# A block-matching convolution kernel: residual addition behind side work, 5x5 convolution in 64x64 tiles, another order of the first image's prologue

## The chip, the cores and the metric

The kernel runs on one core of a Trainium2 chip, as one launch. A core has a matrix engine (TensorE, PE in the profile, with its weight loads as PEld), a vector engine (VectorE, DVE), a scalar engine (ScalarE, ACT), a general engine (GpSimd, POOL) and a queue engine (SyncE, SP). DMAs are issued from POOL, SP or ACT. The engines run their own instruction streams in order and wait for each other through semaphores. The metric is the device time of one execution in microseconds. Before the change it is 6942.3 us, the median of three runs (6939.84 to 6943.18).

## The reference

Eight images of 32 channels and 128x128 pixels, all in f32. Two layers, each of them with a group normalisation ahead and a residual addition behind:

```python
# layer 0
x = x + L0(_gn(x), ...)
# layer 1
x = x + L1(_gn(x), kernel5x5)

def L0(x):
    xb = _patch_match_stack(x)          # for each pixel the 8 best of 25 offsets
                                        # (3x3 patch distance), 8 shifted copies: 256 channels
    dct = _conv(xb, dct_w, groups=C)
    h = relu(_conv(_conv(xb, w1), w2, groups=CK, pad=1))   # 1x1 256->256, depthwise 3x3
    h = relu(_conv(_conv(h, w3), w4, groups=CK, pad=1))
    wiener = sigmoid(_conv(_conv(h, w5), w6, groups=CK, pad=1))
    filt = _conv(wiener * dct, inv_dct_w, groups=C)
    return _conv(filt, agg_w)

def L1(x):                              # one 5x5 kernel for every channel
    return conv(x.reshape(B * C, 1, H, W), kernel, padding=2).reshape(x.shape)
```

`_gn` has 16 groups of two channels: it subtracts the mean of a group and divides by its standard deviation, which is known only when all pixels of the group are there.

## The kernel before

The work is a list of `steps`, (b, n) for image b = 0 to 7 and row group n = 0 to 16. A step s runs, in this order, i = 3, 2, 1, 0: the third 1x1-and-depthwise pair of an older step, the second of the step before, the first of the current step, and the end of the oldest one. For i of 1 to 3, `pointwise_v` makes the half of the 1x1 convolution whose depthwise part is done on DVE (`depthwise_v`: 8 taps of scalar_tensor_tensor on 128x1024, L695, behind a first tap by ACT, L692), and `pointwise_t` makes the half whose depthwise part is done on PE (`depthwise_t`, L718), with DMAs `t<-t` between them. For i = 0, `final_dct` multiplies by the dct of the gathered patches (64x64 matmuls into the two tiles `pc`, L777, then DVE at L785), and `final_add` multiplies by the merged inverse dct and aggregation (`pa`, L798), adds the residual on DVE (L805), takes the statistics of the result (L806) and writes it to `x1d` in DRAM (L810).

Beside these, a step gathers the patches of coming steps in four units. A unit is `gather_load` (DMAs of indices `ib` and of pixels `xt`, issued by POOL), `gather_select` (two ACT operations for each of a number of pairs, L588 and L589) and `gather_pixels` (88 small matmuls `pg`, L603). A unit needs the indices of its quarter of the rows: `ready` holds (b, quarter).

PE, DVE and ACT have a hand-written order: what the Python code emits first runs first. DMAs of POOL and SP are placed by a scheduler. Side work is written as generators, which yield a queue's letter, a cost and, in some places, a number of ticks to wait: "D" work is done by `tick`, four times a step, as far as a credit goes (`total`, spread over the steps of an image); "P", "Q" and "A" are drained at fixed places of the loop; `until` drains all of them until a condition holds. The side work of an image is:

- `prep(b)`: load image b (`load_image`), normalise it (`xn`), form squared differences for the offsets (`df`, L414 and L422, cost `PAIR`), sum over channels (`pd`, L429), sum over patches (`dsum`), take the top 8 (`mx`, `idx`, L506 and L507), turn them to gather indices (`o`, `pi`, `li`, L529 to L540; DRAM tile `idxd`), quarter by quarter.
- `mixes()` and `bands()`, once: matrices made from the small weights (`dq`, `iv`, `ag`, `ldct`, `ib`, `lagg`) and from the 5x5 kernel (`band`, five 128x128 band matrices, one for each dx).
- `layer1(b)`: statistics (L818), then for each of eight chunks of four channels a load `xy` from `x1d` (L837), the normalisation into `xm` (L842, four tensor_scalar), five matmuls `p5` with `band` (L861; an f32 matmul is two instructions), the addition (L872) and the write-out (L873). Two `xy` buffers take turns.

Before the first step, seven gather units are loaded, four of them completed, and a unit of index 3 or less belongs to quarter 0, one of 4 to 7 to quarter 1. Image 0's loads are issued by ACT; SP loads the constants `cst` and all weights. The transposes of w1, w3 and w5 for the 1x1 convolutions are made in a set-up block, in their own PSUM tiles. After it, PSUM has the pools `ps_x` (five banks, tag "x", for pv, p, pg, pc, pa and p5 among others), `ps_dw` and `ps_d`.

In the loop, the `pa` matmuls and the residual addition stand together, after `pointwise_v` of i = 3 in the step that follows:

```python
later()                        # end(): final_add, at the last step of an image push(layer1(b))
later = lambda: None
...
run("Q")
if s < len(steps):
    unit(gather_select, u + 1, (0,))
    unit(gather_load, u + 3)
    tick(b, i)
next(new_v, None)              # taps of depthwise_v on DVE
```

Of the kernel before, what the change touches and what calls it, by code (L numbers as in the profile page):

```python
# [9 lines left out]
F32 = mybir.dt.float32  # L10
# [3 lines left out]
ALU = mybir.AluOpType  # L14
ORDERED = {mybir.EngineType.PE, mybir.EngineType.DVE, mybir.EngineType.Activation}

P = 128
C, K, H, W = 32, 8, 128, 128
# [25 lines left out]
def bm3d_conv_preact(  # L44
# [32 lines left out]

    def load_image(b, engine):

        xn = xnp.tile([P, HR, HX], F32, name=f"xn_{b}", tag="xn")  # L80
        for rg in range(4):
            s = slice(C * rg, C * (rg + 1))
            lo = 32 * rg - 3
            a, z = max(lo, 0), min(lo + HR, H)
            engine.dma_start(xn[s, a - lo : z - lo, 2 : 2 + W], x[b, :, a:z, :])
            for r in range(HR):
                y = lo + r
                if y < 0 or y >= H:
                    y = min(max(y, 0), H - 1)
                    engine.dma_start(  # L90
                        xn[s, r : r + 1, 2 : 2 + W], x[b, :, y : y + 1, :]
                    )
        return xn

    first = load_image(0, nc.scalar)
    cst = const.tile([P, C_N], F32, name="cst")
# [50 lines left out]

    with tc.tile_pool(name="setup", bufs=1) as sp, tc.tile_pool(
        name="setup_ps", bufs=2, space=bass.MemoryType.PSUM
    ) as spp:  # L150
        dwt = sp.tile([P, 3, 4, 9], F32, name="dwt")
        for n, w in enumerate((w2, w4, w6)):
            for g in range(4):
                nc.sync.dma_start(
                    dwt[C * g : C * (g + 1), n],
                    w[:P].rearrange("(q c) o a b -> c q (o a b)", c=C),
                )
            nc.gpsimd.memset(dwd[0:C, n, 1], 0.0)
            for u in range(2):
                for dy in range(3):  # L160
                    s = slice(C * (u + dy), C * (u + dy + 1))
                    nc.gpsimd.tensor_tensor(
                        dwd[s, n, u],
                        cst[s, C_M32 : C_M32 + C]
                        .unsqueeze(1)
                        .unsqueeze(1)
                        .to_broadcast([C, 4, 3, C]),
                        dwt[s, n, :, 3 * dy : 3 * dy + 3].unsqueeze(3).to_broadcast([C, 4, 3, C]),
                        ALU.mult,
                    )  # L170
        wide = {}
        for name, w in (("w1", w1), ("w3", w3), ("w5", w5)):
            t = sp.tile([P, 2, CK], F32, name=f"nat_{name}", tag=f"nat_{name}")
            nc.sync.dma_start(t, w.rearrange("(m p) i a b -> p m (i a b)", p=P))
            if name == "w1":

                nat, t = t, sp.tile([P, 2, CK], F32, name="w1_kc")
                for m in range(2):
                    nc.vector.tensor_copy(
                        t[:, m].rearrange("p (k c) -> p k c", c=C),  # L180
                        nat[:, m].rearrange("p (c k) -> p k c", k=K),
                    )
            wide[name] = t
        for name, dst in (("w1", lw1), ("w3", lw3), ("w5", lw5)):
            for g in range(2):
                ps = spp.tile([P, CK], F32, name=f"ps_{name}_{g}", tag="ps")
                for m in range(2):
                    src = wide[name][:, m, g * P : (g + 1) * P]
                    nc.tensor.transpose(ps[:, m * P : (m + 1) * P], src, ident)
                nc.scalar.copy(dst[:, g], ps)  # L190

# [31 lines left out]
    def run(which, credit=1e9):  # L223

        q, took = queues[which], 0.0
        for _ in range(len(q) if which != "D" else 1000):
# [7 lines left out]
                None,  # L234
            )
            if i is None or took >= credit:
                break
# [16 lines left out]
    def group_stats(mv, name):  # L254
# [19 lines left out]
        return mr  # L274

    def mixes():

# [7 lines left out]
        m8 = work.tile([P, 8], F32, name="m8", tag="m16", bufs=1)  # L285
        yield "D", 1.0
        nc.vector.tensor_reduce(
# [224 lines left out]
    def places(b, idx, i):  # L512
# [4 lines left out]
        yield "D", 2.6  # L517
        o = work.tile([P, 256], F32, name=f"o_{b}_{i}", tag="lin_o", bufs=1)
        ct = work.tile([P, 256], F32, name=f"cn_{b}_{i}", tag="lin_c", bufs=1)
        nc.vector.tensor_copy(  # L520
# [266 lines left out]
    def final_add(b, n, acc, xr, j0, j1):  # L787
# [6 lines left out]
        for m in range(2):  # L794
            for j in range(4):
# [7 lines left out]
                    stop=m == 1,  # L803
                )
        nc.vector.tensor_add(xr, xr, pa)  # L805
        nc.vector.bn_stats(stats[b][:, n], xr)  # L806
# [7 lines left out]
    def layer1(b):  # L814
# [15 lines left out]
        bc = work.tile([P, 2, C], F32, name=f"bc_{b}", tag="bc")  # L830
        nc.scalar.copy(bc.rearrange("p a b -> p (a b)"), pb[:, : 2 * C])
        xys = {}

        def load(c):
            if c < C:
                xys[c] = work.tile([P, 4, W], F32, name=f"xy_{b}_{c}", tag="xy")
                nc.gpsimd.dma_start(xys[c], x1d[b][c : c + 4].rearrange("c y x -> y c x"))  # L837

        def normalise(c):
            xm = work.tile([P, 4, W], F32, name=f"xm_{b}_{c}", tag="xm")  # L840
            for i in range(4):
                nc.vector.tensor_scalar(  # L842
                    xm[:, i],
                    xys[c][:, i],
                    bc[:, 0, c + i : c + i + 1],
                    bc[:, 1, c + i : c + i + 1],
                    op0=ALU.subtract,
                    op1=ALU.mult,
                )
            return xm  # L850

        load(0)
        load(4)
        yield "D", 1.4
        xm = normalise(0)
        for c in range(0, C, 4):
            yield "P", 0
            ps = ps_x.tile([P, 4, W], F32, name=f"p5_{b}_{c}", tag="x")
            for n, dx in enumerate((0, -2, -1, 1, 2)):
                xa, xz = max(0, -dx), min(W, W - dx)  # L860
                nc.tensor.matmul(  # L861
                    ps[:, :, xa:xz],
                    band[:, dx + 2],
                    xm[:, :, xa + dx : xz + dx],
                    start=n == 0,
                    stop=n == 4,
                )
            yield "D", 2.1
            if c + 4 < C:
                xm = normalise(c + 4)  # L870
            xy = xys.pop(c)
            nc.vector.tensor_add(xy, xy, ps)  # L872
            nc.gpsimd.dma_start(out[b, c : c + 4].rearrange("c y x -> y c x"), xy)  # L873
            load(c + 8)

        done.add(b)

# [25 lines left out]
    def end(b, n, xr, j0, j1):  # L903
        final_add(b, n, accs.pop((3, b, n)), xr, j0, j1)
        if n == NS:
            push(layer1(b))

    total = 5.5 + 3.3 + 36 * 1.95 + 4 * 4.6 + 32 * 1.85 + 4 * 2.6 + 8 * 2.1
    owed = [0.0]
# [16 lines left out]
    with tc.manual_schedule(engines=ORDERED):  # L926
        push(prep(0))
        push(mixes())
        xbd[0] = dram.tile([P, 2, H, W], F32, name="xbd_0", tag="xbd")
        for i in range(3):  # L930
            nc.gpsimd.memset(tb[i][0:64, :, 0], 0.0)
        for u in range(7):
            unit(gather_load, u)
            unit(gather_select, u - 2)
            unit(gather_pixels, u - 3)
        u = 4

        dt = dv = kept = iter(())

        later = lambda: None  # L940

        for s in range(len(steps) + 2):
            if s < len(steps):
# [6 lines left out]
                if n == NS - 1 and b + 1 < NB:  # L950
                    until(lambda: b + 1 in ready, 4.0)
                    xbd[b + 1] = dram.tile([P, 2, H, W], F32, name=f"xbd_{b+1}", tag="xbd")
            for i in (3, 2, 1, 0):
                si = s - (i - 1 if i else 2)
# [5 lines left out]
                if live and i:  # L960
# [3 lines left out]
                    accs[i, bi, ni] = [None, next(new_v)]  # L964
                later()
                later = lambda: None
                if live and not i:
# [7 lines left out]

                run("Q")
                if s < len(steps):
                    unit(gather_select, u + 1, (0,))
                    unit(gather_load, u + 3)
                    tick(b, i)  # L980
                next(new_v, None)
                if live and i:
                    pointwise_t(i, bi, ni, lws[i - 1], src)
                next(kept, None)
                if s < len(steps):
                    unit(gather_pixels, u)
                next(dt, None)
                run("A")
                next(dv, None)
                if s < len(steps):  # L990
                    unit(gather_select, u + 1, (1,))
                    u += 1
                next(dt, None)
                kept, dv, dt = dv, new_v, new_t
                if live and not i:
                    later = partial(end, bi, ni, xr, j0, j1)
                if not i and 0 <= s - 1 < len(steps):
                    fins[s - 1] = final_load(*steps[s - 1])
        next(kept, None)
        later()  # L1000
        until(lambda: NB - 1 in done, 4.0)

# [61 lines left out]
```

## Time and profile before

| | us |
|---|---|
| median of three runs | 6942.3 |
| profiled execution | 6939.75 |
| its span, first to last instruction | 6938.0 |
| PE busy | 6488.0 (94%) |
| DVE busy | 5777.4 (83%) |
| ACT busy | 5067.6 (73%) |
| POOL busy | 3018.7 (44%) |
| DVE at L805 waiting for `pa` | 581.2 in 109 waits |
| L861, 640 instructions of the 5x5, busy | 327.6 |
| layer-1 statistics L818, first and last | 1132.8 and 6858.8 |
| first `xbd` write (a step's gathered patches) | 206.8 |

Times in the profile count from the start of the span. A busy share is an average over the span; the row of tenths by slices shows where an engine is full. A wait is listed with the instruction that waited, the one that released it, the total in us, the number of waits and the longest. The granted TensorE clock averages 0.976 over the span.

### The profile page before, as it was taken

How to read it: one execution, taken by the hardware profiler on the slowest of the kernel's cores; microseconds unless marked ns; L12 is line 12 of the kernel's file. 1: busy time of each engine (PE TensorE's matmuls, PEld its weight loads, DVE VectorE, ACT ScalarE, POOL GpSimd, SP SyncE). 2: the span in 40 equal slices, each digit the busy share in tenths (PEclk: the TensorE clock that was granted, in tenths of full speed). 3: DMA queues.
4: the chain of work that ended last, by engine and by line, in shares of the span. 5: the costliest groups of instructions: out<-in, count | busy, mean ns of one | idle time of the engine just before them, and what ended most of it. 6: DMA issues, size and time to landing. Idle time of an engine off the chain costs nothing.

```text
span 6938.0 us, 230820 instructions
## 1 busy us (share of the span) xinstructions
PE 6488.0 (94%) x100450; PEld 3042.2 (44%) x100450; DVE 5777.4 (83%) x8606; ACT 5067.6 (73%) x6698; POOL 3018.7 (44%) x5143
## 2 busy tenths in 40 slices
PE   4699999999999999999999999999999999999997
PEld 1344444444444444444444444444444444444443
DVE  6689988889888898888988898888988889877775
ACT  4687778777687777877777776877768777776772
POOL 6345436334463344534445334553435433333332
PEclk9799999999999999999999999999999999999998
DMA  3566656557565575656756567565666666556652
GB/s 79 132 149 148 156 141 160 147 147 161 144 154 148 137 166 133 162 144 142 162 134 164 142 144 163 142 161 137 152 149 147 165 142 143 143 151 154 156 143 66
DMA packets 774196, 1007.83 MB, mean 145 GB/s; under 512 B 223712, under 2 KB 587168, under 8 KB 773184
## 3 DMA queue, kind: packets, MB, share of 16 engines
q0 software_dynamic: 387104, 733.70, 42.1%
q1 hardware_dynamic: 381056, 256.86, 17.2%
q8 instruction: 791, 12.96, 0.8%
q10 hardware_dynamic: 5024, 2.49, 0.2%
q14 instruction: 221, 1.81, 0.1%
HBM read 542.24 MB, written 217.01 MB: 109 GB/s over the span
## 4 chain that ended last, share of the span: by engine, by line
PE 48%; DVE 23%; issue 8%; DMA 8%; ACT 7%; POOL 5%; SPq 0%; POOLq 0%; DVEq 0%; ACTq 0%
PE pw L718 17%; DVE acc L695 16%; PE pv L641 12%; PE p L665 9%; PE pg L603 3%; PE p L861 3%; DMA t<-t 2%; DVE df L414 2%; PE pc L777 2%; DMA xf<-xbd 2%; DVE idx L507 2%; ACT ib L588 1%; PE pa L798 1%; ACT df L422 1%; DMA dsum<-sq 1%
## 5 line engine op out<-in xcount | busy, mean ns | idle before, releaser
L695 DVE SCALAR_TENSOR_TENSOR acc<-tv,dwv,acc 128x1024 f32<-128x1024 f32 (+3 forms) x3264 | 4031.9, 1237 | 242.1 <-ACT acc L692 126.5
L718 PE MATMUL pw<-t,dwd 96*32 96x508 f32 (+6 forms) x19392 | 2162.2, 592 | 84.7 <-DMA t<-t 58.5
L574 POOL DMA_DIRECT2D ib<-idxd x1024 | 566.7, 554 | 2185.9 <-ACT sel L589 2050.3
L718 PEld LDWEIGHTS pw<-t,dwd 96*32 96x32 f32 (+1 forms) x19392 | 712.3, 112 | 1216.7 <-issue 1135.5
L588 ACT ACTIVATE ib<-ib,nplace 128x1024 bf16<-128x1024 bf16 x1024 | 1170.6, 1143 | 19.1 <-DMA ib<-idxd 19.1
L589 ACT ACTIVATE sel<-ib 128x1024 f32<-128x1024 bf16 x1024 | 1084.5, 1059 | 32.5
L665 PE MATMUL p<-acc,lw 128*32 128x256 f32 x16768 | 981.7, 379 | 5.2 <-ACT tv L649 5.2
L641 PE MATMUL pv<-acc,lw 128*128 128x512 f32 (+1 forms) x2112 | 967.3, 601 | 16.7 <-DVE acc L785 16.0
L758 POOL DMA_DIRECT2D xf<-xbd x1088 | 648.7, 630 | 229.3 <-PE pc L777 121.3
L603 PE MATMUL pg<-sel,xt 128*32 128x48 f32 x45056 | 603.6, 209 | 151.3 <-DVE acc L785 63.7
L665 PEld LDWEIGHTS p<-acc,lw 128*32 128x32 f32 x16768 | 552.8, 111 | 427.2 <-issue 44.9
L649 ACT COPY tv<-pv 128x512 f32<-128x512 f32 (+2 forms) x784 | 438.8, 577 | 408.2 <-PE pv L641 399.4
L603 PEld LDWEIGHTS pg<-sel,xt 128*32 128x32 f32 x45056 | 586.6, 113 | 321.2 <-DVE acc L785 90.5
L422 ACT ACTIVATE df<-df 128x786 f32<-128x786 f32 (+2 forms) x576 | 468.8, 860 | 273.9 <-DVE df L414 271.1
L731 ACT ACTIVATE acc<-pw 128x512 f32<-128x512 f32 (+2 forms) x808 | 440.9, 572 | 268.6 <-PE pw L718 268.2
L641 PEld LDWEIGHTS pv<-acc,lw 128*128 128x128 f32 x2112 | 380.2, 191 | 505.7 <-issue 422.6
L672 ACT COPY t<-p 128x512 f32<-128x512 f32 x800 | 426.0, 571 | 225.1 <-PE p L665 223.0
L699 ACT ACTIVATE acc<-acc 128x1024 f32<-128x1024 f32 (+3 forms) x408 | 416.8, 1022 | 199.4 <-DVE acc L695 199.1
L805 DVE TENSOR_TENSOR xr<-xr,pa 128x256 f32<-128x256 f32 (+2 forms) x136 | 55.0, 404 | 587.3 <-PE pa L798 581.2
L414 DVE TENSOR_TENSOR df<-xn 128x786 f32<-128x786 f32 (+2 forms) x576 | 528.5, 967 | 11.4 <-PE pd L429 10.1
L692 ACT ACTIVATE acc<-tv,dwv 128x1024 f32<-128x1024 f32 (+3 forms) x408 | 454.6, 1114 | 51.7 <-PE pa L798 36.4
L641 PE MATMUL pv<-xb,lw 128*128 128x512 f32 x1024 | 474.3, 606 | 0.0
(128 smaller groups left out, 6041.6 us busy)
## 6 DMA issues: line engine op xcount, KB each, us to landing
ib<-idxd POOLq DMA_DIRECT2D x1024, 256.0 KB, 4.4
xbd<-xb POOLq DMA_DIRECT2D x128, 1024.0 KB, 6.4
xf<-xbd POOLq DMA_DIRECT2D x960, 128.0 KB, 6.6
t<-t SPq DMA_DIRECT2D x792, 128.0 KB
t<-t SPq DMA_DIRECT2D x384, 256.0 KB
tv<-tv SPq DMA_DIRECT2D x384, 130.0 KB
xt<-xtd POOLq DMA_DIRECT2D x240, 176.0 KB, 5.0
xl<-xs POOLq DMA_DIRECT2D x256, 64.0 KB, 2.3
```

The costliest lines, as they stand in the source:

```text
L414: nc.vector.tensor_sub(df[:, :, ca:cz], xn[:, r0 : r0 + SR, ca:cz], xn[:, r0 + dy : r0 + dy + SR, ca + dx : cz + dx],)
L422: nc.scalar.activation(df[:, :, ca:cz], df[:, :, ca:cz], AF.Square)
L574: nc.gpsimd.dma_start(ib.rearrange("p k y x -> p (k y x)"), idxd[b][s4 // 8, s4 % 8, 4 * k0 : 4 * k0 + 8] .rearrange("k x -> (k x)") .part ...
L588: nc.scalar.activation(ib, ib, AF.Square, bias=nplace)
L589: nc.scalar.activation(sel, ib, AF.Relu, scale=-1.0, bias=1.0)
L603: nc.tensor.matmul(pg[C * j : C * (j + 1), :, xa:xz], xt[:, t], sels[j // 2][:, j % 2, :, xa:xz], start=True, stop=True,)
L641: nc.tensor.matmul(ps[:, :hr], lhsT[:, g, P:CK], src(g)[:, h : h + hr], start=g == 0, stop=g == 1,)
L665: nc.tensor.matmul(ps[C * r : C * (r + 1), e, :nb], lhsT[:, g, s], rows[:, r : r + 4 * nb - 3 : 4], start=g == 0, stop=g == 1,)
L692: nc.scalar.activation(acc, rows, AF.Copy, scale=tap)
L695: nc.vector.scalar_tensor_tensor(acc, rows, tap, acc, op0=ALU.mult, op1=ALU.add)
L718: nc.tensor.matmul(pt[u][C * j : C * (j + 1), : nh[u], :nb, xa:xz], dwd[0:hi, i - 1, u, j, dx + 1], t[0:hi, j, : nh[u], :nb, xa + dx : xz ...
L758: nc.gpsimd.dma_start(xf[p : p + C, m, j0:j1], src[g, m, (h + m + 1) % 2, :, :, ya:yz])
```

## The change

Seven things are changed together.

1. `load_image(0)` takes two issuers in turn, ACT and SP, a row group each, ahead of the constants.
2. The transposes of w1, w3 and w5 leave the set-up block: `weights()` makes them as side work, in `acc` tiles and `ps_x` banks, after 8 ticks; `mixes` waits 10 ticks. While image 0 isn't ready, `run("D")` takes other work before squared differences.
3. Before step 0 only the four units of quarter 0 run; step 0 runs none, steps 1, 2 and 3 run 4, 4 and 8, each beginning with loads of its own quarter. From then on it is one unit for each i, as before.
4. `final_add` yields between the matmuls and the addition; the addition, the statistics and the `x1d` writes follow after the select, load and tick of the same place.
5. The tiles `lin_o` and `lin_c` become one tile that shares the buffer of tag "v".
6. The 5x5 takes eight channels at a time, as two groups e of four, and the two halves h of the rows apart: four 64x64 tiles of the array, two PSUM banks. For e = 1 the halves of the output change places, so a second copy with exchanged halves is loaded (two DMAs) and normalised. Rows 62 to 65, which need both halves, aren't written from there: `middle(b)` computes them on DVE from its own loads. Normalisation waits three ticks after the loads, the next load one tick after the write-out. The costs in `total` change with it.
7. In the last image all four chunks are loaded at once into buffers that are free by then, and a chunk is normalised before the addition of the one ahead.

The core of the diff:

```diff
-    first = load_image(0, nc.scalar)
+    first = load_image(0, nc.scalar, nc.sync)
...
+            if which == "D" and 0 not in ready:
+
+                i = next((k for k, (c, _, at) in enumerate(q) if at <= now[0] and c != PAIR), i)
...
+    def weights():
+
+        natural, kc = {}, None
+        for i, (name, w) in enumerate((("w1", w1), ("w3", w3), ("w5", w5))):
+            t = accp.tile([P, 2, R * W // 2], F32, name=f"nat_{name}", tag=f"acc{i + 1}0")
+            natural[name] = t = t[:, :, :CK]
+            nc.sync.dma_start(t, w.rearrange("(m p) i a b -> p m (i a b)", p=P))
+        yield "D", 1.0, 8
...
-        yield "D", 1.0
+        yield "D", 1.0, 10
...
-        o = work.tile([P, 256], F32, name=f"o_{b}_{i}", tag="lin_o", bufs=1)
-        ct = work.tile([P, 256], F32, name=f"cn_{b}_{i}", tag="lin_c", bufs=1)
+        oc = work.tile([P, R, W + 2], F32, name=f"oc_{b}_{i}", tag="v", bufs=1)
...
+        yield
         nc.vector.tensor_add(xr, xr, pa)
         nc.vector.bn_stats(stats[b][:, n], xr)
...
+            nc.gpsimd.dma_start(t[0], src[:, c : c + 4])
+            for h in range(2):
+                nc.gpsimd.dma_start(
+                    t[1][64 * h : 64 * h + 64], src[64 - 64 * h : P - 64 * h, c + 4 : c + 8]
+                )
+            nc.gpsimd.dma_start(t[2], src[:, c + 4 : c + 8])
...
+            for k, dx in enumerate((0, -2, -1, 1, 2)):
                 xa, xz = max(0, -dx), min(W, W - dx)
-                nc.tensor.matmul(
-                    ps[:, :, xa:xz],
-                    band[:, dx + 2],
-                    xm[:, :, xa + dx : xz + dx],
-                    start=n == 0,
-                    stop=n == 4,
-                )
-            yield "D", 2.1
...
+                for h in range(2):
+                    for e in range(2):
+                        r, o = 64 * h, 64 * ((h + e) % 2)
+                        nc.tensor.matmul(
+                            ps[e][o : o + 64, :, xa:xz],
+                            band[r : r + 64, dx + 2, r : r + 64],
+                            t[3 - 2 * e][r : r + 64, :, xa + dx : xz + dx],
+                            start=k == 0,
+                            stop=k == 4,
+                        )
+            yield "D", 3.6 if last else 1.6
+            if last and c + 8 < C:
+                normalise(c + 8)
+            for e in range(2):
+                y = t[2 * e]
+                nc.vector.tensor_add(y, y, ps[e])
+                for a, z in ((0, 62), (66, P)):
+                    nc.gpsimd.dma_start(
+                        out[b, c + 4 * e : c + 4 * e + 4, a:z].rearrange("c y x -> y c x"),
+                        y[a:z],
+                    )
+            if c + 8 < C and not last:
+                yield "A", 0, 1
+                load(c + 8)
...
+    def middle(b, mr):
...
+        yield "D", 2.6, 4
+        nc.vector.tensor_copy(acc, df[:, 2, 2 : 2 + W])
+        nc.vector.tensor_scalar(
+            df[:, 0:5, 2 : 2 + W],
...
+        for dy in range(5):
+            if dy in (2, 4):
+                yield "D", 2.0
+            for dx in range(5):
+                nc.vector.scalar_tensor_tensor(
+                    acc,
+                    df[:, dy, dx : dx + W],
+                    kb[:, 5 * dy + dx : 5 * dy + dx + 1],
...
-        for u in range(7):
-            unit(gather_load, u)
-            unit(gather_select, u - 2)
-            unit(gather_pixels, u - 3)
-        u = 4
...
+        begin(0)
+        u = 0
+        while u < 4:
+            u = whole(u, 4)
...
+            count = {0: (0, 0, 0, 0), 1: (2, 2, 0, 0), 2: (2, 2, 0, 0), 3: (2, 2, 2, 2)}
+            count = count.get(s, (1, 1, 1, 1)) if s < len(steps) else (0, 0, 0, 0)
+            limit = 4 * (s + 1) if s < 3 else len(units)
+            if 0 < s < 4:
+                begin(u)
...
-                later()
-                later = lambda: None
+                next(later, None)
...
                     tick(b, i)
+                next(later, None)
                 next(new_v, None)
```

## Prediction

> **What bounds the kernel now.** I read the page's sections 1, 2 and 5 first, then the busy times in stretches, then the waits, and the chain of waits for the last 90 us.
>
> ```profile
> PE 6488.0 (94%) x100450; PEld 3042.2 (44%) x100450; DVE 5777.4 (83%) x8606; ACT 5067.6 (73%) x6698; POOL 3018.7 (44%) x5143
> PE   4699999999999999999999999999999999999997
> PEclk9799999999999999999999999999999999999998
> ...
> L805 DVE TENSOR_TENSOR xr<-xr,pa 128x256 f32<-128x256 f32 (+2 forms) x136 | 55.0, 404 | 587.3 <-PE pa L798 581.2
> ```
>
> TensorE (PE) is the bound except in the first two slices and the last: elsewhere its row shows nines. VectorE (DVE) does not look like a bound at 83%, but it lost 581.2 us in 109 waits at one line, the residual addition waiting for its `pa` matmuls. The stretches show where each engine is the limit (columns: stretch, length, then busy PE, PEld, DVE, ACT, POOL, clock, DMA share, GB/s):
>
> ```profile
> 0.00:50.00 50.00, 5.79 (x22) 4.24 (x22) 10.03 (x27) 6.15 (x17) 26.98 (x41) 1.00 0.45 77
> 50.00:100.00 50.00, 36.13 (x192) 9.85 (x192) 43.18 (x46) 36.21 (x51) 39.83 (x59) 0.97 0.32 62
> 150.00:200.00 50.00, 20.42 (x398) 10.59 (x398) 27.06 (x115) 25.12 (x31) 18.45 (x31) 0.64 0.26 57
> 1600.00:1700.00 100.00, 96.86 (x1542) 45.49 (x1534) 94.99 (x209) 77.75 (x103) 47.00 (x82) 1.00 0.80 182
> 1132.80:1950.80 818.00, 785.95 (x12386) 371.00 (x12380) 713.57 (x1063) 618.29 (x819) 365.85 (x624) 0.99 0.63 151
> ```
>
> The fifth line is one image: the layer-1 statistics (L818) come at 1132.8 first and 6858.8 last, and (6858.8 - 1132.8)/7 = 818.0 us per image. PE works 786 of these 818, DVE 714. The fourth line shows that near a place DVE is at 95%: the two are close. The first 50 us wait for the image; at 150 to 200 no engine is busy and the clock is 0.64. The first convolution matmul starts at 232.35. The last stretch is a ring of waits (start, length, what):
>
> ```profile
> 6862.86 3.33 DMA xy<-x1d
> 6866.28 1.13 DVE xm L842 x4
> 6867.55 6.96 PE p L861 x10
> 6875.51 2.71 DMA out_dram<-xy
> 6878.50 3.11 DMA xy<-x1d
> 6904.11 4.52 issue
> 6908.64 2.71 DMA out_dram<-xy
> 6912.39 4.47 issue
> ```
>
> A buffer's write-out must land before the next load, and that before the next matmuls: 8.2 us per chunk of four channels (6908.64 - 6900.36). From the last statistics to the end it is 6938.0 - 6858.8 = 79 us.
>
> [...] in `pc` (L777) 64x64 matmuls of 512 columns, four tiles in turn, cost 245.5 us for 1984, 124 ns each, or 0.495 us per group of four, where one 128x128 matmul of the 5x5 (L861) costs 35.85/80 = 0.448. [...] the new 5x5 writes both banks from both row halves, but so does `pc`, at that price. [...] the ring above idles PE so, and its 80 matmuls take 44.84 us at clock 0.86 against 35.85. [...] the image's big loads are issued from 0.75 to 30.3 us.
>
> **The change part by part.**
>
> *5x5 in 64x64 tiles.* Today 8 channels are 20 matmul instructions: 20 x 0.448 = 8.96 us. Afterwards they are 40, ten groups of four: 10 x 0.495 = 4.95 by the form of `pc`. Gain 4.0 per 8 channels, 16 us an image. Bounds: 10 x 0.448 (gain 18), and no overlap of the two row halves (gain 0). With PE busy 786 of 818 a matmul saved is time saved, so I take 16 x 7 = 112 for the seven images inside the pipeline; the eighth belongs to the tail.
>
> *Middle rows on DVE.* A 64-row tile misses its neighbours' rows, so `middle` recomputes rows 62 to 65: 25 scalar_tensor_tensor on 128x128, for which the trace has 351 ns (L695's small form), 25 x 0.351 = 8.8; one tensor_scalar over 640 elements, about 0.8 by (1024 - 640) elements less than L695's 1.28; a copy, 0.25. That is 9.9 us an image, DVE 714 -> 723. [...] 351 for 128 and 1284 for 1024 elements leave 218 ns fixed here, so 25 small ones are dear. Cover: the 72 us an image (581.2/8) that DVE sits at L805. Without that cover it would cost up to 9.9 x 7 = 69.
>
> *Residual addition later.* The matmuls `pa` stay behind `pointwise_v`; the addition, its bn_stats and four x1d writes now follow the tick's side work on DVE. It removes waits of 581.2/136 = 4.3 us a step from DVE. PE is not behind that wait at once, so most is slack; what PE got from it are waits for DVE, `PE pg L603 <- DVE acc L785` 63.7 us in all and its like, some 8 to 15 us an image of the 32 that PE idles. I take 3 an image for seven (21), and 15 once for image 0, where 550 to 860 us runs at DVE's pace and a 50 us share of the wait lies (300 to 1100). Queued behind the addition now: taps of `depthwise_v` on DVE, and on POOL the x1d writes. One of the five `ps_x` banks is held for a tick longer, and two go to a 5x5 pair. Bounds: +1 us a step if PE then waits for a bank (+136), -8 us an image if all the idle goes (-56).
>
> *DMAs.* Each image gets per chunk of 8 two half loads and two more outs (8 more in 4 chunks less the coarser ones, about 24 with `middle`): at 0.75 us of POOL's issue time, 18 us on an engine with 366 of 818 busy. Nothing, by that slack; if a gather load is late behind them, 0.75 each.
>
> *Prologue.* Loads of image 0 go out on ACT and SP alternately and first; constants, weight loads (7 + 12 + 3 + 32 on SP) follow. Big loads start by 3 us instead of up to 30.3, so the image lands at about 20 instead of 40.8 (start of bn_stats), estimated from 2.3 MB at the 135 to 150 GB/s bursts of that stretch. The side chain (squares, distances, top-8) then starts some 20 us earlier, but meets the `dq` loads late in SP's queue (5 us). Weight transposes leave the set-up. The first gather needs one quarter of the rows' indices, not two: instead of seven units, four precede step 0. First convolution: I get 137 against 232.35. This isn't the gain: the DVE work of quarters 1 to 3 is only moved between steps 0 to 3, where each step waits for a whole quarter. Busy DVE in 0 to 350 is 233 us, idle 117; in the new order I count the holes (image 20, `dq` 5, before the first taps 23, before steps 1, 2 and 3 14, 12 and 8, smaller ones 5) as 87. Gain 30. Bounds: 5, if each quarter's chain takes the 20.2 and 25.3 us waits seen today at its end; 70, if step 0's matmuls fill them all.
>
> *Tail.* All four chunks' loads (12 x 0.75 on POOL) go out at once behind the last x1d write into buffers of their own. From 6862.9: first pair normalised 6868.6; the four 5x5 pairs end near 6877, 6882, 6887 and 6894, the last normalisation (8 x 0.286) and the middle rows between them on DVE; last additions 6897.7, outs 3 more to issue, 2.7 to land, 0.8 close: 6904. Gain 34. [...] Bounds 22 (every chunk cold, mid loads late) and 42.
>
> Sum on the profiled execution, which took 6939.75 with a span of 6938.0: 112 + 21 + 15 + 30 + 34 = 212, hence 6938 - 212 = 6726, and 6728 with what lies around the span. The median shown, 6942.3, is 2.5 above the profiled run: 6730.
>
> **Rivals.**
>
> *A. DVE becomes the bound (0.22).* The period is then set by DVE's chain, which gets 9.9 longer while the waits at L805 turn into waits elsewhere (for ACT's seed of `acc`, 126.5 today). For: 95 of 100 at 1600 to 1700. Against: the 818 period has 104 idle on DVE. The pipeline's gain falls to about 6 an image: 42 + 30 + 34 = 106, hence 6836.
>
> *B. All gains are full (0.2).* Ten groups at 0.448 (126), 8 us an image of PE's idle (56), 25 in image 0, prologue 60, tail 40: 307, hence 6635. Against: PE idles also for `t` DMAs (58.5), which nothing here touches.
>
> *C. Slower (0.06).* [...] Then the 40 instructions cost 0.448 each: 17.9 against 8.96, +8.96 x 4 x 7 = +251, and the +36 of the tail eat its gain; minus 66 from the addition and the prologue, +185: 7127. Against: `pc` at 124 ns. It decides from 40 x t > 20 x 0.448 + 2 (66/28 us per chunk = 2.4), t about 0.28 us.
>
> *D. The change doesn't do what it says (0.04).* The wait at L805 is moved, not removed, banks are short, and the prologue's holes only move; then only tail and half the 5x5: about 6850.
>
> **How the numbers follow.** Forecast 0.48, A 0.22, B 0.2, C 0.06, D 0.04. The range takes 6620 to 6845: from B's end to A and a part of D. A measurement of this kernel tells about 0.2%, 14 us, from no change. Faster 0.92, same 0.02 (D shrunk further), slower 0.06.
>
> **What would show each step.** L818's spacing: 800 is the forecast, 812 A, 790 B, over 840 C. The 5x5's busy time per image: 18 to 20 us, or 70 for C. L805's wait: under 100 us in all. First L641 matmul: near 137, with xbd of step 3 some 30 us earlier. Last L818 to the end: 45 us. It is wrong if PE's waits for DVE or for PSUM banks grow by more than 5 us an image, or if DVE's idle in the first 350 us stays over 110.

## The result and the profile after

The changed kernel takes 6892.9 us (median of four runs) against 6942.7 for the kernel before on the same chip: a ratio of 0.9933 with a 95% interval of 0.9918 to 0.9948, 50 us less. The forecast was 212 less. The profiled execution has a span of 6891.4 us. Its page, the same parts as were shown of the kernel before:

```profile
PE 6367.0 (92%) x101090; PEld 2974.7 (43%) x101090; DVE 5860.0 (85%) x8822; ACT 5064.3 (73%) x6698; POOL 3247.1 (47%) x5351
...
PE   4599999999999999999999999999999999999997
...
PEclk8799999999999999999999999999999999999998
DMA packets 809531, 1019.84 MB, mean 148 GB/s; under 512 B 255456, under 2 KB 619936, under 8 KB 808512
```

PE works 121 us less (6488.0 before), but the span shrank by 47 only. The 5x5 itself works 145 us less, 150.3 us in place of 295.7 (its line in the trace before; the 327.6 of the table isn't found there). Of these, 125 are in the seven images inside the pipeline, where 126 was the better bound. So other matmuls took 24 us longer, 19 of them the unchanged `pc` (254.7 before, 273.9 now); why is not shown. PE's share fell from 94% to 92%: it idles more. POOL works 228 us more, and there are 35,335 more DMA packets (774,196 before), 31,744 of them under 512 bytes. The wait at the residual addition is smaller, not gone, in the groups of the changed kernel (line, operation, count, busy, mean ns, idle before):

```profile
L817 DVE TENSOR_TENSOR xr<-xr,pa 128x256 f32<-128x256 f32 (+2 forms) x136 | 54.7, 402 | 346.9 <-PE pa L809 332.3 <-DMA xbd<-xb 11.5 <-DMA xf<-xbd 2.7
```

The best marks for a comparison of stretches are the writes of a step's gathered patches (`xbd<-xb`), 16 an image in the same order in both kernels. I take the sixth one of an image (n = 5), which lies behind all of the prologue, and the last one of the run:

| stretch | before | changed | difference | forecast |
|---|---|---|---|---|
| start to n = 5 of image 0 | 424.3 | 450.6 | +26.3 | -30 |
| from there to the last write | 6322.7 | 6263.3 | -59.4 | -148 (112 + 21 + 15) |
| from there to the end of the span | 191.0 | 177.5 | -13.5 | -34 |

All three missed. The first has the wrong sign, the second is 40% of the forecast, the third the same. From these marks comes also the steady period, the mean of the five intervals from image 1 to image 6: 839.7 us before (836.2 to 842.9), 827.3 in the changed kernel. It isn't the 818 of the forecast: that mean over seven took in the last interval, 711 us, in which no next image is prepared. A period is read from one profile of each kernel. Its intervals spread by 7 us before, and executions of one kernel by some 30 us, so 1 to 3 us of a period show little by themselves.

### The profile page after: what moved, and what is told of

It reads as the page before. It is cut to its first block, busy times and chain, and to the rows that moved or that the text cites. A ratio compares the mean times of both kernels' runs of the same rounds, so it can differ in the third digit from the quotient of the medians.

```text
span 6891.4 us, 232427 instructions
## 1 busy us (share of the span) xinstructions
PE 6367.0 (92%) x101090; PEld 2974.7 (43%) x101090; DVE 5860.0 (85%) x8822; ACT 5064.3 (73%) x6698; POOL 3247.1 (47%) x5351
## 3 DMA queue, kind: packets, MB, share of 16 engines
q1 hardware_dynamic: 383568, 258.11, 17.0%
## 4 chain that ended last, share of the span: by engine, by line
PE 52%; DVE 21%; ACT 9%; DMA 9%; issue 6%; POOL 3%; SPq 0%; ACTq 0%; POOLq 0%; DVEq 0%
PE pw L729 18%; DVE acc L706 13%; PE pv L652 13%; PE p L676 11%; DMA t<-t 5%; PE pg L614 3%; ACT ib L599 2%; PE pc L788 2%; PE p L902 2%; DVE df L424 2%; ACT df L432 2%; DVE idx L517 1%; DVE acc L796 1%; PE pa L809 1%; PE pd L439 1%
## 5 line engine op out<-in xcount | busy, mean ns | idle before, releaser
L729 PE MATMUL pw<-t,dwd 96*32 96x508 f32 (+6 forms) x19392 | 2159.6, 592 | 148.9 <-DMA t<-t 107.0
L676 PE MATMUL p<-xb,lw 128*32 128x256 f32 x8192 | 467.6, 380 | 0.2 <-DVE xy L914 0.2
```

The costliest lines, as they stand in the source:

```text
L676: nc.tensor.matmul(ps[C * r : C * (r + 1), e, :nb], lhsT[:, g, s], rows[:, r : r + 4 * nb - 3 : 4], start=g == 0, stop=g == 1,)
L729: nc.tensor.matmul(pt[u][C * j : C * (j + 1), : nh[u], :nb, xa:xz], dwd[0:hi, i - 1, u, j, dx + 1], t[0:hi, j, : nh[u], :nb, xa + dx : xz ...
```

## Experiments

The differences above suggested two causes, apart from each other: the prologue's order, and something in the DMAs of the tiled 5x5. The kernel before took 6911 to 6953 us in all these runs, so every kernel is compared with it by the ratio on the same chip; the steady period is from its profile.

**The gather order of before, in the changed kernel.**

```diff
-        begin(0)
-        u = 0
-        while u < 4:
-            u = whole(u, 4)
+        for u in range(7):
+            unit(gather_load, u)
+            unit(gather_select, u - 2)
+            unit(gather_pixels, u - 3)
+        u = 4
...
-                more = count[3 - i]
```

> The changed kernel with the gather order of before: seven units loaded and four completed ahead of step 0, then one for each i; loads on two issuers, weights as side work and the rest stay as changed. Theory 1: the prologue loses because, step by step, a whole quarter's chain (squares, distances, top 8, indices, gather) must end before the next step, with nothing of the next quarter beside it. Then this gets back the 26 us that the steps of image 0 came late, and some 20 more since the image still lands early: 6892.9 - 46 = 6847 (6835 to 6865). Rival: the loss comes from the loads behind dq, the weights or the order of side work; then it stays at 6885 to 6900.

Measured: 6847.95, ratio 0.9879 (0.9854 to 0.9904), and n = 5 of image 0 at 403.2 in place of 450.6. So the new order alone cost 47 us there, and the rest of the new prologue (loads on two issuers, weights as side work) gained 21 against the kernel before. Over the whole run the two ratios are 37 us apart, with intervals that do not overlap. The profile of the changed kernel shows the hole. First DVE, then PE, in order of time (start, length, operation, idle before it and what ended that):

```profile
106.69 3.62 DVE L424 TENSOR_TENSOR df<-xn 128x786 f32<-128x786 f32 x4
138.31 3.65 DVE L424 TENSOR_TENSOR df<-xn 128x792 f32<-128x792 f32 x4 [28.00 <-PE pd L439]
```

```profile
106.82 0.69 PE L549 MATMUL pi<-cst,oc 128*128 128x128 f32 x2 [9.01 <-DVE oc L540]
117.46 0.38 PE L614 MATMUL pg<-sel,xt 128*32 128x48 f32 x4 [9.94 <-DMA xt<-xtd]
...
133.30 1.92 PE L614 MATMUL pg<-sel,xt 128*32 128x48 f32 x84 [1.75 <-ACT sel L600]
136.67 3.75 PE L439 MATMUL pd<-df,neg 128*32 128x393 f32 x16 [1.44 <-ACT df L432]
```

DVE has differences of quarter 1 to form, but their buffers come free only when PE has read them (`pd`), and `pd` stands in PE's order behind the four units of quarter 0. PE waits there first for the indices from DVE (9.01 us) and the pixel load (9.94), then within each unit for ACT's selection (1.75). From 100 to 150 us DVE works 17.9 of 50 us.

**Quarter 1 ahead of the first units.** The changed kernel's gather order, with write-outs as in the whole write-outs below, and one line more:

```diff
         begin(0)
+        until(lambda: (0, 1) in ready, 4.0)
         u = 0
```

> The changed kernel's gather order with whole write-outs, and the side work of quarter 1 ended ahead of the first four units. Its distance matmuls then stand ahead of the units' matmuls in PE's order, so VectorE does not wait 28 us for them. Theory: the 46 us that the new order loses are such waits at each quarter, and this undoes the first of them: 10 to 25 us of 46 come back, ratio 0.9735 to 0.976 against 0.9774. Rival: the quarters' chains are serial whatever stands first, and the time stays at 0.977 to 0.979.

Measured: 0.9736 (0.972 to 0.9752) against 0.9774 (0.9756 to 0.9793); n = 5 at 429.1 against 449.2. The first of the waits is gone, and it was worth 20 of the 46 us. What DVE waits for in its first 400 us (total, times, longest) changes so, first the changed kernel, then this one:

```profile
DVE df L424 <- PE pd L439: 52.4, 5, 28.0
DVE acc L706 <- ACT acc L703: 27.0, 4, 11.9
DVE mx L516 <- ACT ct L509: 16.3, 7, 5.4
```

```profile
DVE mx L516 <- ACT ct L509: 38.9, 7, 18.8
...
DVE df L424 <- PE pd L439: 13.2, 4, 11.7
```

Removing one wait uncovers the next, at the top 8 of a quarter. The other 26 us remain; that they are the later quarters' waits of the same kind is argued, not tried.

**Image 0 by one issuer**, with the old gather order and whole write-outs:

```diff
-    first = load_image(0, nc.scalar, nc.sync)
+    first = load_image(0, nc.scalar)
```

> Old gather order and whole write-outs, with image 0 loaded by ACT alone as before. Theory: the early landing of the image (bn_stats at 17 us in place of 41) is what brings the steps 21 us forward; without it they are as late as before: ratio 0.9696 + 0.0030 = 0.9726 (0.971 to 0.975). Rival: it is hidden behind the weights and the loads of dq, and the early steps come from the weight transposes off the set-up: 0.969 to 0.971.

Measured: 0.9732 (0.9716 to 0.9748) against 0.9696 (0.9672 to 0.9719); the intervals overlap a little. n = 5 is at 415.2 in place of 403.4, so two issuers are worth 12 of the 21 us at that mark. In the profiled execution the later images made up for it (span 6724.6 against 6723.6), but it was the fastest of its four (6726.4 to 6750.9), so the end-to-end worth stays open.

**The residual addition alone**, in the kernel before:

```diff
+        yield
         nc.vector.tensor_add(xr, xr, pa)
...
                     tick(b, i)
+                next(later, None)
                 next(new_v, None)
```

> The kernel before with the later residual addition alone. Theory: DVE's wait at the addition was slack behind PE, so it is worth nothing or little: 6928 to 6945. Rival (the prediction's term): 21 + 15 less, 6906. Rival 2: the statistics of an image come later (14 us in the changed kernel's trace) and a bank is held: 6950 to 6960.

Measured: 0.9966 (0.9952 to 0.9979), 23 us less; between the theory and the forecast's term. The period falls by 5.5, from 839.7 to 834.2.

**The tiles alone**, in the kernel before: chunks of eight, `middle`, the last image's loads, the shared index tile and the costs (the diff of points 5 to 7 above).

> The kernel before with the 5x5 in 64x64 tiles, the middle rows, the last image's loads and the shared index tile alone; prologue and residual addition as before. Theory: PE-bound, 17.9 us of PE an image less over seven images and 14 in the tail, less 3 to 5 an image: 6942.7 - 110 = 6833 (6820 to 6850). Rival: VectorE's middle rows cost the period as much as they do in the changed kernel (12 of 18 kept): 6942.7 - 90 - 14 = 6845. Rival 2: DVE's new work isn't covered without the later addition: 6870 to 6890.

Measured: 0.9988 (0.9979 to 0.9997), period 841.1. All three expectations fell: 18 us of PE an image went and the period did not fall at all. VectorE's busy time rose by 9.5 us an image, which can't take all 18, so the rest was looked for in the DMAs.

**Whole write-outs**, in the changed kernel:

```diff
-                for a, z in ((0, 62), (66, P)):
-                    nc.gpsimd.dma_start(
-                        out[b, c + 4 * e : c + 4 * e + 4, a:z].rearrange("c y x -> y c x"),
-                        y[a:z],
-                    )
+                nc.gpsimd.dma_start(
+                    out[b, c + 4 * e : c + 4 * e + 4].rearrange("c y x -> y c x"), y
+                )
...
+        while (b, 0) not in done:
+            yield "A", 0, 1
         for r in range(4):
             nc.gpsimd.dma_start(out[b, :, 62 + r], acc[C * r : C * (r + 1)])
```

> The changed kernel with write-outs of all 128 rows, one DMA for four channels as before, and middle's rows written over them afterwards. The 62-row write-outs take 1.50 us each of POOL's issue, 16 an image, 24 us, against 8 of 0.76. Theory: that is slack inside the pipeline and costs in the tail alone: 6892.9 - 15 = 6878 (6870 to 6885). Rival: POOL's issue time delays loads in every image too: 18 us an image less of POOL, 3 to 6 us an image less of the period: 6835 to 6860. Rival 2: the middle's write-outs must now wait for all others at the end, and the gain is under 5: 6888 to 6895.

Measured: 6777.45, ratio 0.9774 (0.9756 to 0.9793), some 110 us less than the changed kernel and more than any expectation. The period falls from 827.3 to 814.5, and the last stretch of the table from 177.5 to 158.3. So other work doesn't cover the 62-row write-outs. The DMA views (size, median us from issue to landing) differ so, first the changed kernel, then this one:

```profile
out_dram<-xy POOLq DMA_DIRECT2D x112, 124.0 KB, 10.6
```

```profile
out_dram<-xy POOLq DMA_DIRECT2D x56, 256.0 KB, 3.1
```

Of the 117 us between the two profiled spans 36 are PE's busy time (6367.0 and 6331.3 us for as many instructions, at a mean granted clock of 0.969 and 0.975), and 81 are PE's idle time. Whether the lower clock is only a consequence of the waits is not shown.

**Quarter write-outs**: the same with four DMAs of 32 rows in place of the one.

> The changed kernel with write-outs of all 128 rows as four DMAs of 32 rows for each four channels, middle's rows written over them. POOL then issues 32 an image, estimated at 0.5 us each from the 32-row x1d writes: 16 us an image against 24 for the 62-row ones and 6 for the whole ones[...]. Theory A: what cost the 115 us is POOL's issue time; then more than half of it comes back: ratio to the kernel before 0.984 to 0.989. Theory B: it is the slow landing of the 62-row writes (10.6 us against 3.1), for which later DMAs of POOL wait; then the ratio stays at that of the whole write-outs, 0.976 to 0.980.

Measured: 0.9797 (0.9771 to 0.9823), period 815.4. POOL's busy time is 3202.0, 101 us above the whole write-outs, and the period is 0.9 us longer, too little to tell: POOL's issue time in sum is slack, as the forecast had it. That left the form of the 62-row DMA.

**Which row counts are slow.** Old gather order; all rows written as two DMAs, cut at another row in each chunk:

```diff
+                if c == 8:
+                    nc.gpsimd.dma_start(o4[:62], y[:62])
+                    nc.gpsimd.dma_start(o4[62:], y[62:])
+                if c == 16:
+                    nc.gpsimd.dma_start(o4[:60], y[:60])
+                    nc.gpsimd.dma_start(o4[60:], y[60:])
...
```

> Old gather order, write-outs of all rows as two DMAs for each four channels, cut at another row in each chunk of eight channels: 64 + 64 rows, 62 + 66, 60 + 68, 56 + 72; middle's rows written over them. A measurement: issue on POOL and landing by number of rows. Theory: [...] 62 rows land in some 10 us, 68 in 5 to 8, the others in 2.5 to 4. Rival: any count other than a multiple of 16 (or of 32) lands slowly, 60, 66 and 72 like 62. Rival 2: the number of bytes or DMAs decides, and 62 and 64 land alike.

Measured in one execution, 6738.5 us. Its DMA view gives the size (2 KB a row) and the median time to landing:

```profile
out_dram<-xy POOLq DMA_DIRECT2D x28, 128.0 KB, 3.1
out_dram<-xy POOLq DMA_DIRECT2D x14, 144.0 KB, 3.4
out_dram<-xy POOLq DMA_DIRECT2D x14, 136.0 KB, 5.3
out_dram<-xy POOLq DMA_DIRECT2D x14, 132.0 KB, 8.0
out_dram<-xy POOLq DMA_DIRECT2D x14, 124.0 KB, 9.3
out_dram<-xy POOLq DMA_DIRECT2D x14, 120.0 KB, 3.0
out_dram<-xy POOLq DMA_DIRECT2D x14, 112.0 KB, 3.0
```

and its lines give POOL's issue time (min, median, max in ns) for 62, 66, 60 and 68 rows:

```profile
L920 POOL DMA_DIRECT2D out_dram<-xy x14: 1509/1540/1584, 1314.8 to 6143.9; - x14
L921 POOL DMA_DIRECT2D out_dram<-xy x14: 716/744/757, 1316.4 to 6145.4; - x14
L923 POOL DMA_DIRECT2D out_dram<-xy x14: 662/682/725, 1394.2 to 6204.1; - x14
L924 POOL DMA_DIRECT2D out_dram<-xy x14: 1090/1101/1123, 1394.9 to 6204.8; - x14
```

60 and 56 rows are as fast as 64, so it isn't a multiple of 16 or 32 that matters; 62 rows are slow in landing (9.3) and issue (1.54), 68 rows are in between (5.3 and 1.10). The other issue times are short: 64 rows 0.64, 60 rows 0.68, 56 rows 0.70, 66 and 72 rows 0.74. Landings are as expected but for 66 rows (8.0): this DMA was always issued 1.5 us behind a 62-row one, and may have stood behind it; that was not tried by itself. What in a row count decides is not shown: the slow ones are known from these times alone.

**The same rows in fast pieces**, in the changed kernel, rows 62 to 65 left out as there:

```diff
-                for a, z in ((0, 62), (66, P)):
+                for a, z in ((0, 48), (48, 62), (66, 80), (80, P)):
```

> The changed kernel with each 62-row write-out cut in 48 and 14 rows: the same rows and bytes, rows 62 to 65 left out as in the change, twice as many DMAs, each on a row count that landed fast. Theory: [...] the ratio goes from 0.9933 to that of the quarter write-outs, 0.977 to 0.983. Rival: leaving out or ordering the middle rows, or the number of DMAs, had a share; then 0.985 to 0.993.

Measured: 0.9779 (0.9762 to 0.9795), period 815.3, landings 2.4 us (48 rows) and 2.3 (14 rows). The same bytes in twice as many DMAs take back what the whole write-outs do (0.9774): the loss came from the form, and no share of the overwritten middle rows or their order can be told from zero.

**Who passes the delay on.** Both forms again, issued by SP, so that POOL has nothing of them. Theory C is that the write-outs make SP's copies slow, whoever issues them:

```diff
-                    nc.gpsimd.dma_start(
+                    nc.sync.dma_start(
                         out[b, c + 4 * e : c + 4 * e + 4, a:z].rearrange("c y x -> y c x"),
```

> The changed kernel with the same 62-row write-outs, issued by SP in place of POOL. POOL's 24 us an image and its waits for the landings are gone; the DMAs are as many and as long, and stand in SP's order among the t and tv copies. Theory A (issue time) and B (POOL's waits for landings) expect the ratio of the whole write-outs, 0.977 to 0.981, if SP's copies aren't held up; theory C[...] expects no gain, 0.990 to 0.995; SP's copies held up: above 0.995.

> Write-outs of 48 and 14 rows issued by SP. The 62-row write-outs on SP took 1.0008, with POOL free of them. Theory C: [...] then the fast form on SP gains as much as on POOL, 0.977 to 0.985. Rival: SP's t copies stood in the queue behind write-outs that wait for VectorE; then it stays at 0.995 to 1.003.

Measured: 62 rows on SP 1.0008 (1.0 to 1.0017), 48 and 14 rows on SP 0.9787 (0.977 to 0.9803). So the form costs on either queue, and that write-outs stand in SP's order is not the reason by itself. But the first run doesn't tell slow copies from copies that wait in SP's queue: one 62-row write-out holds SP's issue for 2.9 us (min, median, max in ns), with copies `t<-t` behind it in the same queue. First 62 rows, then 48 and 14:

```profile
L916 SPq DMA_DIRECT2D out_dram<-xy x112: 241/2925/7874, 1293.2 to 6447.3; - x112
```

```profile
L916 SPq DMA_DIRECT2D out_dram<-xy x224: 326/404/1609, 1292.7 to 6316.9; - x112
```

The packets of SP's queue show what moved. Its count is 383,568 with the write-outs on POOL, 415,568 with 62 rows on SP and 419,152 with 48 and 14 rows. 128 write-outs of 62 rows and four channels are 31,744 packets of 512 bytes, one for each row, so none was split there. What is left over are packets of 4 bytes: 256, or 2 for each 62-row DMA, and 3,840, or 30 for each pair of 48 and 14 rows. So the slow form has fewer packets than the fast one. On POOL, too, the data of a 62-row DMA go in whole packets, 30 of 4 KB and 2 of 2 KB; 224 of 32 or 16 bytes come with them, and what these do is not shown.

In the changed kernel the write-outs are POOL's and the copies SP's, in two queues, and still the copies are slow; what they share that slows them is not shown. I took the packets of the 256 KB copies from the trace, 256 at a time in order of time. A copy that starts within 12 us behind the issue of a 62-row write-out takes 6.5 us from its first packet to its last (median of 29), any other 2.6. With 48 and 14 rows on POOL it is 3.8 and 2.6, with whole write-outs 2.7 and 2.6. PE's waits for the copies show where it arrives; in turn the changed kernel, whole write-outs, 62 rows on SP, and 48 and 14 rows on SP:

```profile
PE pw L729 <- DMA t<-t: 107.0, 43, 7.7
```

```profile
PE pw L729 <- DMA t<-t: 68.3, 28, 7.8
```

```profile
PE pw L729 <- DMA t<-t: 177.8, 53, 7.2
```

```profile
PE pw L729 <- DMA t<-t: 60.6, 24, 7.4
```

On POOL, later DMAs of the changed kernel wait for the landing besides (total, times, longest):

```profile
POOL xy L863 <- DMA out_dram<-xy: 88.2, 13, 9.2
POOL xf L769 <- DMA out_dram<-xy: 56.5, 37, 4.2
```

With whole write-outs the first of these is 26.3 us, and the second isn't there. How the 110 us divide between the two ways was not told apart.

**Tiles with whole write-outs**, in the kernel before, with its own prologue and residual addition:

> The kernel before with the 5x5 in 64x64 tiles, middle rows and last image's loads, and write-outs of all 128 rows. The tiles alone gave 0.9988. Theory: the write-outs hid their gain; then the predicted term appears: 17.9 us of PE for seven images and 25 to 30 in the tail, 0.980 to 0.984. Rival: VectorE's middle rows take half of it without the later addition: 0.986 to 0.990.

Measured: 0.9814 (0.9789 to 0.9839), period 826.4, last stretch 158.1. The predicted terms of the tiles and the tail appear: 13.3 us an image and 33 at the end. With the later addition on top (the whole write-outs run above) the period is 814.5, another 11.9: by these single profiles the addition is worth twice as much with the tiles as alone (5.5).

**Without the middle's taps**, with old gather order and whole write-outs:

```diff
-        for dy in range(5):
-            if dy in (2, 4):
-                yield "D", 2.0
-            for dx in range(5):
-                nc.vector.scalar_tensor_tensor(
...
+        yield "D", 2.0
+        yield "D", 2.0
```

> Old gather order and whole write-outs, with the 25 taps of the middle rows left out (rows 62 to 65 then hold the layer's input alone). 8.8 us of VectorE an image are gone. Theory: TensorE sets the period and the taps are covered: 0 to 2 us an image, ratio 0.9675 to 0.970. Rival (case A of the prediction): VectorE is the bound by now, and 5 to 9 us an image come back: 0.960 to 0.965.

Measured: 0.9671 (0.9654 to 0.9688) against 0.9696, overlapping; the period 810.9 against 814.2. VectorE's busy time fell by 65.9 us, 8.2 an image. At most about 3 of these are on the path, which is within the spread of the periods; the rest is covered.

**Both faults removed.** Old gather order with whole write-outs, and with 48 and 14 rows:

> Both edits together on the changed kernel: gather order of before, and write-outs of all 128 rows. If the two losses are apart (prologue 45 us in its own run, write-outs 115), the time is 0.983 x 0.988 of the changed kernel or 160 us less: ratio to the kernel before 0.970 (0.968 to 0.973). Rival: they share a cause, and the ratio stays above 0.975.

> The same with the gather order of before. Theory: both losses removed, 0.969 to 0.975. A candidate for the best version, since its last writes needn't wait for the others.

Measured: 6720.45, 0.9696 (0.9672 to 0.9719), and 6740.43, 0.9717 (0.9701 to 0.9733). Both beat the kernel before and the changed one; they aren't told apart. The page of the first:

```profile
PE 6317.0 (94%) x101090; PEld 2956.2 (44%) x101090; DVE 5854.9 (87%) x8822; ACT 5054.4 (75%) x6698; POOL 3102.1 (46%) x5287
...
PE   4798899999999999999999999999999999999998
```

0.9696 of 6942.7 is 6732. Its stretches against the kernel before are 403.4 (-21), 6159.6 (-163) and 160.6 (-30), where the forecast had -30, -148 and -34. That the sum comes out at the forecast's 212 is in part luck: the tiles and the prologue gave less than their terms, the residual addition more.

## Why the prediction was wrong

- *"DMAs. ... Nothing, by that slack."* This step failed, and it carries most of the miss. It priced a write-out at 0.75 us of POOL's time, the price of a 128-row write-out, and asked only whether POOL had slack. POOL had it (quarter write-outs: 101 us more of POOL, no period lost that can be told). But a 62-row DMA is another form than a 128-row one: 1.5 us to issue (the 128-row one 0.76 to 0.82 before), 10.6 to land in this kernel in place of 3.1, with SP's copies late behind it (6.5 us in place of 2.6). It cost about 13 us of each image's period and 19 us of the last stretch. The bound kept for it ("0.75 each") could not contain that. The row count was in the diff.
- *"Prologue ... Gain 30."* The second step that failed. The image lands even a little earlier than forecast (bn_stats from 16.4), and the first convolution matmul runs at 140.35, against 137. The sum of holes was off: DVE idles 118 us of the first 350, as before, where 87 were counted. Missing was the wait behind PE's order, 28 us at `df` for `pd`, and, as argued above, like waits of the later quarters. The order of side work cost 47 us, the other parts gained 21.
- *"5x5 in 64x64 tiles", 16 an image.* Right in mechanism. The three chunks between 1174 and 1500 us take 13.45 us of PE for 120 instructions, 0.448 per group of four, the better bound; with fast write-outs the period fell by 13.3. The 18 us an image that this saves in the 5x5 do not all arrive, and `pc`, which took 254.7 us before and 280.0 in that run, takes back 3. Case C, 40 instructions at 0.448 each, didn't occur: they took 13.45/120 = 0.112.
- *"Middle rows on DVE", cover of 72 us.* Mostly right: at most about 3 of 8.2 us an image show.
- *"Residual addition later", 3 an image.* Under-sized: 5.5 alone, 11.9 with the tiles. That DVE's idle at L805 is less of a slack when PE has 18 us an image less to do fits this, but was not tried by itself. 332 of 581 us of that wait are still there, where under 100 was named.
- *"Tail", 34.* Right as to the loads: from the last statistics to the end it is 47.6 us with whole write-outs (45 was named for it), though the loads are 16 and not the 12 that were counted. In the changed kernel it is 64.7: sixteen write-outs at 1.5 us, and the last of them lands late, in the chain of waits:

```profile
6849.99 6.41 POOL out_dram L916 x5
...
6862.16 17.43 DMA out_dram<-xo
```

- *The cases.* The time landed above the range, beyond case A, but A's reason did not hold: VectorE is not what took the gain. The forecast's own list asked whether PE's waits for DVE or PSUM banks grew; it did not ask for PE's waits for DMAs, which did (58.5 to 107.0 at `t<-t`). Case B even named these 58.5 us as what nothing here touches; the write-outs touched them.

## What to carry to other kernels

A DMA's price isn't its bytes or its issue time alone: 62 rows landed in 9.3 us where 60 rows took 3.0, and copies behind 62-row writes took 6.5 where others took 2.6. So a changed row count must be priced as a new form, with what it delays in other queues. When a prologue is cut in stages, write down for each stage what stands ahead of its producers in every in-order engine; an early first step is worth nothing if the next stage's producer waits behind it. An engine's idle time that is slack today can become worth something when the bound engine has less to do: the later addition brought 5.5 us of the period alone and 11.9 with the tiles.

## What was not expected of the hardware

A write of 62 rows (124 KB) took 9.3 to 10.6 us to land and 1.5 us to issue, one of 60 rows (120 KB) 3.0 and 0.68. On SP one held the queue's issue for 2.9 us, and sixteen an image there, with POOL free of them, took away all that the rest of the change had gained (1.0008). And 64x64 tiles in an accumulating chain over two banks ran at 0.448 us per group of four (13.45/30), as one 128x128 matmul of the kernel before does (35.85/80).
